# Where layer 0's weights are queued, four normed tiles in layer 1, and four banks for early keys

## The chip, the cores and the metric

The kernel runs on one core of a Trainium2 chip. The core has five engines that each work through their own list of instructions in order: TensorE (PE, with its weight loads PEld), VectorE (DVE), ScalarE (ACT), GpSimd (POOL) and SyncE (SP, which here only issues transfers). They wait for each other through semaphores. ACT, SP and POOL also issue DMA transfers: an instruction in the engine's list starts one, and if that instruction has to wait, everything behind it in the list waits too.

The metric is the device time in microseconds, the median of three runs.

## The reference

A batch of 4 sequences of 256 tokens with 256 features goes through four layers. Each layer is a cross attention to a context of 1601 tokens per sequence and then a feed-forward part, both added to `x`, each on the layer norm of `x`.

```python
x = x + _L0_xattn_ref(_layernorm(x), ctx_2048, mask)
x = x + _L0_ffn_ref(_layernorm(x), ...)      # 32 experts, 8 chosen for each token
x = x + _L1_xattn_ref(_layernorm(x), ctx_2048, ...)   # a decayed mean of the context
x = x + _L1_ffn_ref(_layernorm(x), ...)      # 8 experts, 2 chosen, and a shared expert
x = x + _L2_xattn_ref(_layernorm(x), ctx_2048, ...)   # 16 heads, 4 key-value heads
x = x + _L2_ffn_ref(_layernorm(x), ...)      # 4 experts, 1 chosen
x = x + _L3_xattn_ref(_layernorm(x), ctx_2048, ...)   # 32 heads
x = x + _L3_ffn_ref(_layernorm(x), ...)      # quantized to three weight values
```

Three of these parts matter here. The expert layers 0 and 1 compute, for every token, a weighted sum of the outputs of a few chosen experts, `silu(x Wg) * (x Wu)` times `Wd`. And layer 2's attention needs keys and values of the context, which depend only on the context and not on `x`:

```python
k_ctx = (h_ctx_kv @ wk_ctx).reshape(B, T, NUM_KV_HEADS, HEAD_DIM)
v_ctx = (h_ctx_kv @ wv_ctx).reshape(B, T, NUM_KV_HEADS, HEAD_DIM)
k_ctx = rms_norm(k_ctx, k_norm_w)
```

## The kernel before

**Stages.** The stages run in the order of the layers: layer 0's attention (0 to 141 us in the profile), layer 0's router and token sort (141 to 231), its expert tiles (231 to 376), the way back of its results (376 to 498), layer 1's norms, router, shared expert and expert tiles (498 to 624), their way back (624 to about 668), and from there layer 2's attention, whose first scores come at 694.75. Layer 1's attention is only a mean and two layer norms, and is done inside layer 0's way back.

**An expert layer** works in five steps. `normed` (L106) makes the layer norm of each of the four sequences: VectorE writes a tile `xn` of 128 x 512, ACT issues a write of it to memory (`xd`, L114), PE transposes it into a bank `tp_ln` and VectorE or ACT (in turn, `evac`) copies that to `xnT`. The tiles `xn` come from a pool of two, so the third norm can be written only when the first tile's write to memory has landed. Then the router's products give logits; VectorE finds the chosen experts (`match_replace`, a one-hot `oh`), and `slots` (L524) counts with two products how many tokens each expert has. One-hot products on PE in four parts sort the tokens (L383 to L403). For each tile of 128 sorted tokens, POOL gathers the rows of `xd` by an indirect DMA, PE transposes them, multiplies with the expert's weights, and the result is written to `yd`. There are 95 such tiles in layer 0 and 23 in layer 1. On the way back POOL gathers for each 128 tokens the rows of their chosen experts from `yd` (8 gathers in layer 0, 2 in layer 1) and VectorE adds them to `x` with their gates (L515, L860).

**Layer 0's weights** are two tensors of 32 experts, `w13` (6 MB) and `w2` (3 MB). Eight parts of four experts are loaded by 16 DMAs in a loop ahead of the norms (L337 to L339), all from ACT's list. In the compiled program every DMA from ACT or SP signals on one of eight semaphores in turn, and waits, before it is issued, for the landing of the earlier one on the same semaphore.

**Early keys.** Layer 2's context keys and values of 15 of the 16 pairs of sequence and head group (units) are made ahead of time, as filling work for PE. `l2_early` (L1169) is a generator; each `next` on it, by `fill(n)` (L101), puts one step in. A unit has 7 product steps and 4 turn steps, 11 in all. A product step is four matmuls of two context tiles of 128 rows into one PSUM bank; ACT copies the keys out (`kr_early`, L1200) and the values (`va_early`, six buffers, L1201), and SP stores the values (`vd`). After the seventh, ACT squares the keys (`sq_early`, one buffer), VectorE sums the squares (`ss_early`, L1212), and the keys are scaled (L1216, on `self.scaler`: VectorE on the ways back, otherwise POOL). The turn steps transpose the keys of the unit before on PE, ACT copies them out (`kT_early`, three buffers, L1227), and SP stores them (`kd`). How many steps go where is written in the tables `F0`, `G0`, `F1` and `G1`: 9 for each of the nine rounds of layer 0's way back, 3 for each of the ten of layer 1's.

**PSUM.** In the expert layers eight banks are in four pairs: `tp` and `tpf` (pool `psf`), `gu` (`psg`), `y` (`psy`). The bank of a filling step comes from `self.take`, here the pair `tpf`. The expert tiles use `y` for the last product (`f0y`, `f1y`).

**Order.** A scheduler places each engine's instructions by its own estimate of when they are ready. Those given to `pin` keep their order in the program. It does not follow the text line by line, so an edit can move other instructions as well.

**Into layer 2.** `l2_xattn` (L1245) first loads a mask, a norm weight and rotary tables (L1267 to L1276) from SP's list, and multiplies the tables with the norm weights on VectorE. The tile `wb` has one buffer, so the second of its loads waits until VectorE has used the first. Then come the norm of the first sequence (transposes L1297) with two filling steps, its query products with the remaining ones, and the scores.

Of the kernel before, what the change touches and what calls it, by code (L numbers as in the profile page):

```python
# [11 lines left out]
F32 = mybir.dt.float32  # L12
# [11 lines left out]
P = 128  # L24
B = 4
S = 256
NT = B * S
D = 256
# [8 lines left out]
E0, I0, K0 = 32, 96, 8  # L37
# [3 lines left out]
NH2, NKV2, HD2 = 16, 4, 128  # L41
# [7 lines left out]
F1 = [1, 2, 2, 3]  # L49
G1 = 3  # L50
LN2, Q2, C2 = 2, 2, 6
# [7 lines left out]
class Kernel:  # L59
    def __init__(self, ctx, tc, ins, out):  # L60
        self.ctx, self.tc, self.nc = ctx, tc, tc.nc
        self.i, self.out = ins, out
        self.flip = 0


# [32 lines left out]
    def pin(self, ins):  # L98
        self.tc.keep_in_program_order(ins)

    def fill(self, n):  # L101

        for _ in range(n):
            next(self.early, None)

    def normed(self, ps, fills, xd=None):  # L106


        xT = [self.xnT.tile([P, 2, 512], F32, name=f"xnT{tb}", tag="xnT") for tb in range(2)]
        for b in range(B):  # L110
            xn = self.xn.tile([P, 2, D], F32, name="xn")
            self.layernorm(xn, self.x[b])
            if xd is not None:
                self.nc.scalar.dma_start(xd.rearrange("(b q p) d -> b p q d", p=P, q=2)[b], xn)  # L114
# [199 lines left out]
    def l0_ffn(self, one):  # L314
# [7 lines left out]
        nc, tc = self.nc, self.tc  # L322
# [9 lines left out]
        with ExitStack() as es:  # L332
# [3 lines left out]
            w2 = wp.tile([I0, E0, D], F32, name="f0w2")  # L336
            for e in range(0, E0, 4):  # L337
                nc.scalar.dma_start(w13[:, e : e + 4], self.i["l0_w13"][:, e : e + 4])
                nc.scalar.dma_start(w2[:, e : e + 4], self.i["l0_w2"][:, e : e + 4])  # L339
            src = rt.tile([P, NS], U32, name="f0src")  # L340
# [5 lines left out]
            nc.gpsimd.tensor_scalar(start, tok[:, 0:1], float(P), None, ALU.mult)  # L346
            xT = self.normed(ps, F0[:B], xd)


            lg = products()[:, : 8 * E0].rearrange("p (t e) -> p t e", e=E0)  # L350
            for t in range(8):
                for k in range(2):
                    self.mm(lg[:, t, :], xT[t // 4][:, k, (t % 4) * P : (t % 4 + 1) * P], wr[:, k, :], k == 0, k == 1)
            self.fill(F0[B])
            self.l1_summary()
            l = rt.tile([P, 8, E0], F32, name="l0_l")
# [6 lines left out]
            nc.vector.tensor_single_scalar(oh, oh, GONE, ALU.is_equal)  # L363
            cum, end = self.slots(rt, "f0", E0, oh, products(), low, keep, lambda: self.fill(F0[B + 1]))

            cum1 = rt.tile([P, E0, 8], F32, name="f0cum1")
# [16 lines left out]
            for part in range(4):  # L383
                ones = []
                for t in range(2 * part, 2 * part + 2):
# [9 lines left out]
                    ones.append((t, rows, cols))  # L395
                self.fill(F0[B + 2])
                for t, rows, cols in ones:
                    for r in range(K0):
# [97 lines left out]
    def l0_add(self, two, weights):  # L496
# [3 lines left out]
        slot, gate, yd = self.back0  # L500
        self.scaler = nc.vector
        rows = []
        for t in range(9):
# [16 lines left out]
            if t > 5:  # L520
                next(weights, None)
        self.scaler = nc.gpsimd

    def slots(self, pool, name, ne, oh, ct, low, keep, meanwhile):  # L524
# [126 lines left out]
    def l1_ffn(self, weights):  # L651
# [11 lines left out]
        with ExitStack() as es:  # L663
# [27 lines left out]
            def shared_expert():  # L691

                last = None
                for t in range(9):
# [9 lines left out]
                    if last is not None:  # L704
                        u, h = last
                        tp = ps.tile([P, 3, P], F32, name="f1tps", tag="tp")
                        hT = two.tile([P, 3, P], F32, name="f1hTs")
                        y = ps_y.tile([P, D], F32, name="f1y", tag="y")
                        for m in range(3):
# [116 lines left out]
            def down(n, hT):  # L826
                y = ps_y.tile([P, D], F32, name="f1y", tag="y")
                for m in range(2):
# [16 lines left out]

            self.scaler = nc.vector
            rows = []
            for t in range(10):
# [7 lines left out]
                if t > 1:  # L856
                    xt = self.x[(t - 2) // 2][:, (t - 2) % 2, :]
                    for r in range(K1):
# [4 lines left out]
                        )  # L863
                self.fill(G1)
            self.scaler = nc.gpsimd
# [379 lines left out]
    def l2_xattn(self):  # L1245
# [11 lines left out]
        with ExitStack() as es:  # L1257
# [12 lines left out]
            nc.sync.dma_start(kw, i["l2_knw"].rearrange("o p -> p o"))  # L1270
            tabs = {}
            for n, src, nt in (("l2_qnw", "rope_q", 2), ("l2_knw", "rope_k", 3)):
                rope = one.tile([P, 2, nt, HD2], F32, name=src, tag="qt2", bufs=2)
                nc.sync.dma_start(rope, i[src])
                wb = one.tile([P, HD2], F32, name=n + "b", tag="wb")
                nc.sync.dma_start(wb, i[n].to_broadcast([P, HD2]))  # L1276
                ra = one.tile([P, nt, HD2], F32, name=n + "ra")
# [937 lines left out]
```

## Time and profile before

The profile shows one execution on the chip. Its own time is 2638.45 us.

| What | Value |
|---|---|
| median of three runs | 2638.49 us (2635.17 to 2639.96) |
| profiled execution, its own time | 2638.45 us |
| profiled execution, span from first to last instruction | 2636.7 us |
| mean granted TensorE clock | 0.974 of full speed |
| filling products on PE (`fill<-wkc_early,ctxT`) in the whole span | 189.6 us in 780 rows, two rows for a matmul |
| ACT, stage 376 to 498: idle until a key store has landed (before L1227) | 13.4 us |
| POOL, stage 376 to 498: gathers of layer 0's way back (L506) | 64, from 381.3 to 472.6 us, 3.1 us each to landing |
| loads of layer 0's weights | 8 of 768 KB and 8 of 384 KB |
| loads of layer 1's expert weights (`l_w`) | 6 of 704 KB |

How to read the lines that follow: in the page, each digit of a row is the busy share of one of 40 equal slices of 66 us, in tenths; PEclk is the clock granted to TensorE. In the view by windows a line is a stretch of time, its length, the busy time of each engine with the number of instructions, the granted clock, the busy share of the DMA engines and GB/s. In the timeline a line is a start, a duration, an engine (ACTq and SPq are transfers issued from that engine's list), a source line, the operation and what it writes and reads; in brackets stands how long the engine was idle before it and what ended that. In the view of waits a line is who waited for whom, how long in total, how often, and the longest.

### The profile page before, as it was taken

How to read it: one execution, taken by the hardware profiler on the slowest of the kernel's cores; microseconds unless marked ns; L12 is line 12 of the kernel's file. 1: busy time of each engine (PE TensorE's matmuls, PEld its weight loads, DVE VectorE, ACT ScalarE, POOL GpSimd, SP SyncE). 2: the span in 40 equal slices, each digit the busy share in tenths (PEclk: the TensorE clock that was granted, in tenths of full speed). 3: DMA queues.
4: the chain of work that ended last, by engine and by line, in shares of the span. 5: the costliest groups of instructions: out<-in, count | busy, mean ns of one | idle time of the engine just before them, and what ended most of it. 6: DMA issues, size and time to landing. Idle time of an engine off the chain costs nothing. (4 is left out here: it accounts for less than half of the span.)

```text
span 2636.7 us, 47077 instructions
## 1 busy us (share of the span) xinstructions
PE 2491.9 (95%) x17816; PEld 1517.6 (58%) x17816; DVE 1480.0 (56%) x3039; ACT 1310.9 (50%) x2957; POOL 750.8 (28%) x1030
## 2 busy tenths in 40 slices
PE   7989988898799999999999999998998999999997
PEld 4668967676455555555555555655564544545553
DVE  6344637644587777777777777673334414333323
ACT  2334545433644445444544454442326766757775
POOL 1015646123334343334443434431102001011000
PEclk8989999999999999999999999998999999999998
DMA  5154787615511111111111110004211100000000
GB/s 201 60 199 128 186 174 216 205 56 174 162 38 46 39 37 46 46 38 47 46 46 46 46 46 21 9 1 159 87 66 63 34 2 27 4 3 2 6 6 5
DMA packets 94655, 186.25 MB, mean 71 GB/s; under 512 B 15052, under 2 KB 62864, under 8 KB 93232
## 3 DMA queue, kind: packets, MB, share of 16 engines
q1 hardware_dynamic: 78118, 141.36, 15.8%
q0 software_dynamic: 10416, 28.46, 5.0%
q10 hardware_dynamic: 5898, 13.41, 1.5%
q8 instruction: 145, 2.38, 0.4%
q14 instruction: 78, 0.64, 0.1%
HBM read 136.77 MB, written 46.42 MB: 69 GB/s over the span
## 5 line engine op out<-in xcount | busy, mean ns | idle before, releaser
L1471 ACT ACTIVATE p<-s,nm 128x448 f32<-128x448 f32 (+1 forms) x512 | 326.9, 645 | 423.9 <-DVE nm L1467 259.1
L1932 ACT ACTIVATE e<-s 128x1024 f32<-128x1024 f32 (+1 forms) x448 | 404.2, 960 | 160.8 <-PE s L75 156.1
L75 PE MATMUL s<-kT,qT 128*32 128x448 f32 (+1 forms) x4096 | 470.2, 556 | 10.0 <-ACT p L1471 5.0
L75 PE MATMUL o<-pT,va 128*128 128x256 f32 (+2 forms) x1920 | 432.5, 377 | 6.1 <-DVE pT L1513 6.1
L1507 POOL TENSOR_SCALAR p<-p,rm 128x448 f32<-128x448 f32 (+1 forms) x512 | 323.7, 657 | 369.6 <-DVE rm L1500 339.4
L75 PEld LDWEIGHTS o<-pT,va 128*128 128x128 f32 (+1 forms) x1920 | 345.4, 191 | 93.6 <-issue 51.5
L1513 DVE STREAM_TRANSPOSE pT<-p 128x896 f32<-128x896 f32 (+1 forms) x256 | 283.8, 1127 | 37.1 <-POOL p L1507 33.4
L1467 DVE TENSOR_REDUCE nm<-s 128x2 f32<-128x896 f32 (+1 forms) x256 | 282.6, 1104 | 3.4
L75 PE MATMUL s<-qb,kT 32*128 32x256 f32 (+1 forms) x3328 | 267.7, 405 | 11.0 <-ACT e L1932 11.0
L75 PEld LDWEIGHTS s<-kT,qT 128*32 128x32 f32 x4096 | 123.6, 109 | 265.0 <-issue 222.5
L75 PE MATMUL o<-e,va 128*32 128x256 f32 (+1 forms) x3328 | 236.6, 392 | 1.2 <-DVE os L2029 1.2
L75 PEld LDWEIGHTS s<-qb,kT 32*128 32x128 f32 (+1 forms) x3328 | 163.1, 181 | 105.5 <-issue 75.8
L75 PE MATMUL fill<-wkc_early,ctxT 128*128 128x256 f32 x780 | 189.6, 401 | 11.8 <-ACT kT_early L1227 9.6
L75 PEld LDWEIGHTS fill<-wkc_early,ctxT 128*128 128x128 f32 x780 | 152.1, 199 | 43.1 <-ACT kT_early L1227 15.0
L75 PEld LDWEIGHTS o<-e,va 128*32 128x32 f32 (+1 forms) x3328 | 90.8, 110 | 115.5 <-issue 75.5
L1959 POOL TENSOR_TENSOR x<-x,t 128x32 f32<-128x32 f32 x64 | 14.7, 252 | 439.7 <-DVE t L1954 439.7
L1464 DVE TENSOR_TENSOR s<-s,mask 128x128 f32<-128x128 f32 (+1 forms) x256 | 83.1, 325 | 67.1 <-PE s L75 62.3
L410 POOL DMA_INDIRECT f0xr<-f0xd,f0src x95 | 92.3, 972 | 51.3 <-PE f0tph L467 43.2
L1359 POOL TENSOR_TENSOR qo<-qo,qt 128x512 f32<-128x512 f32 x32 | 40.7, 1273 | 230.6 <-DVE rm L1500 139.4
L1471 ACT ACTIVATION_READ_ACCUMULATOR p<-s,nm 128x1 f32 x512 | 101.7, 199 | 0.0
L1200 ACT COPY kr_early<-fill 128x256 f32<-128x256 f32 (+1 forms) x105 | 37.3, 355 | 97.9 <-PE fill L75 97.7
L75 PE MATMUL f2gu<-f2wgu,f2xsT 128*128 x176 | 84.3, 603 | 0.6 <-ACT f2xsT L72 0.3
(510 smaller groups left out, 3503.7 us busy)
## 6 DMA issues: line engine op xcount, KB each, us to landing
ctxT<-in_ctxT SPq DMA_DIRECT2D x10, 1664.0 KB
f0yd<-f0ys SPq DMA_DIRECT2D x95, 128.0 KB
vd<-va_early SPq DMA_DIRECT2D x90, 128.0 KB
kd<-kT_early SPq DMA_DIRECT2D x45, 256.0 KB
kT<-kd SPq DMA_DIRECT2D x15, 768.0 KB
va<-vd SPq DMA_DIRECT2D x15, 768.0 KB
wq<-in_l_wq SPq DMA_DIRECT2D x16, 512.0 KB
wo<-in_l_wo SPq DMA_DIRECT2D x16, 512.0 KB
```

What stands on the lines that cost most here:

```text
L75: self.nc.tensor.matmul(out, lhsT, rhs, start=start, stop=stop, **kw)
L410: nc.gpsimd.indirect_dma_start(out=t, out_offset=None, in_=xd[:, :], in_offset=bass.IndirectOffsetOnAxis(ap=src[:, n : n + 1], axis=0),)
L1200: nc.scalar.copy(kr[:rows, m : m + n, :], tp[:rows, :n, :HD2])
L1359: nc.gpsimd.tensor_tensor(o1, o1, t2, ALU.add)
L1464: nc.vector.tensor_tensor(sv, sv, mask[:, 2 * c : 2 * c + 2, : nt - CT, :].rearrange("p n t i -> p n (t i)"), ALU.add)
L1467: nc.vector.tensor_reduce(nm[:, 2 * c : 2 * c + 2], s[:, :, : nt * 32], AX.X, ALU.max, negate=True)
L1471: nc.scalar.activation(p[:, n, : nt * 32], s[:, n, : nt * 32], AF.Exp, bias=nm[:, e : e + 1], accum_out=sm[:, e : e + 1],)
L1507: nc.gpsimd.tensor_scalar(p[:, n, : nt * 32], p[:, n, : nt * 32], r[:, e : e + 1], 1.0, ALU.mult, ALU.mult)
L1513: nc.vector.transpose(pT[:, 2 * c : 2 * c + 2, :nt, :].rearrange("p n t i -> p n (t i)"), p[:, :, : nt * 32])
L1932: nc.scalar.activation(e[:kr, :, :n, :], s[t][:kr, :, :n, :], AF.Exp, scale=1.0 / math.sqrt(HD3))
L1959: nc.gpsimd.tensor_tensor(xt, xt, t[:, q], ALU.add)
```

## The change

- Layer 0's 16 weight loads leave their place ahead of the norms. A generator `load` issues them in eight parts of two, the even parts from ACT's list and the odd ones from SP's, all pinned. Two parts are put in behind the norms, two behind the router's products, two behind the slot counts, and the last two in the first two rounds of the sort.
- `normed` takes a pool. In layer 1 this is the pool `f1r`, with four buffers for `xn`; layer 0 keeps two.
- `wide_take` hands out four banks for filling steps in turn, the pair `tpf` and the pair `y`. It is used in both ways back. The tiles `y` are declared 512 wide, a whole bank, with the same number of buffers.
- `G1` becomes a table: 9 steps in the first round of layer 1's way back, then 3 three times, then 2. The sum stays 30.
- The six loads of layer 2's mask and tables move from SP's list to ACT's.

```diff
-G1 = 3
+G1 = [9, 3, 3, 3, 2, 2, 2, 2, 2, 2]
...
+    def wide_take(self):
+
+        self.flip4 = not self.flip4
+        if self.flip4:
+            return self.psf[0].tile([P, 512], F32, name="fill", tag="tpf")
+        return self.psf[2].tile([P, 512], F32, name="filly", tag="y")
...
-            xn = self.xn.tile([P, 2, D], F32, name="xn")
+            xn = pool.tile([P, 2, D], F32, name="xn", bufs=B) if pool else self.xn.tile([P, 2, D], F32, name="xn")
...
-            for e in range(0, E0, 4):
-                nc.scalar.dma_start(w13[:, e : e + 4], self.i["l0_w13"][:, e : e + 4])
-                nc.scalar.dma_start(w2[:, e : e + 4], self.i["l0_w2"][:, e : e + 4])
+            def load():
+
+                for n, e in enumerate(range(0, E0, 4)):
+                    queue = nc.sync if n % 2 else nc.scalar
+                    self.pin(queue.dma_start(w13[:, e : e + 4], self.i["l0_w13"][:, e : e + 4]))
+                    self.pin(queue.dma_start(w2[:, e : e + 4], self.i["l0_w2"][:, e : e + 4]))
+                    yield
...
             xT = self.normed(ps, F0[:B], xd)
+            next(loads)
+            next(loads)
...
             self.fill(F0[B])
+            next(loads)
+            next(loads)
             self.l1_summary()
...
             cum, end = self.slots(rt, "f0", E0, oh, products(), low, keep, lambda: self.fill(F0[B + 1]))
+            next(loads)
+            next(loads)
...
                 self.fill(F0[B + 2])
+                next(loads, None)
...
-                y = ps_y.tile([P, D], F32, name="f0y", tag="y")
+                y = ps_y.tile([P, 512], F32, name="f0y", tag="y")[:, :D]
...
+        take = self.take
+        self.take = self.wide_take
...
-            xT = self.normed(ps, F1[:B], xd)
+            xT = self.normed(ps, F1[:B], xd, rt)
...
+            self.take = self.wide_take
...
-                self.fill(G1)
+                self.fill(G1[t])
...
-            nc.sync.dma_start(mask, i["mask2"])
+            nc.scalar.dma_start(mask, i["mask2"])
...
-                nc.sync.dma_start(rope, i[src])
+                nc.scalar.dma_start(rope, i[src])
```

More of the change, by code (lines that the diff above doesn't have):

```diff
@@ L63, in __init__ @@
         self.flip = 0
+        self.flip4 = False
     def evac(self, out, in_):
@@ L104, in fill, with normed @@
             next(self.early, None)
-    def normed(self, ps, fills, xd=None):
+    def normed(self, ps, fills, xd, pool=None):
         xT = [self.xnT.tile([P, 2, 512], F32, name=f"xnT{tb}", tag="xnT") for tb in range(2)]
         for b in range(B):
-            xn = self.xn.tile([P, 2, D], F32, name="xn")
+            xn = pool.tile([P, 2, D], F32, name="xn", bufs=B) if pool else self.xn.tile([P, 2, D], F32, name="xn")
             self.layernorm(xn, self.x[b])
-            if xd is not None:
-                self.nc.scalar.dma_start(xd.rearrange("(b q p) d -> b p q d", p=P, q=2)[b], xn)
+            self.nc.scalar.dma_start(xd.rearrange("(b q p) d -> b p q d", p=P, q=2)[b], xn)
             self.fill(fills[b])
@@ L336, in l0_ffn @@
             w2 = wp.tile([I0, E0, D], F32, name="f0w2")
-            for e in range(0, E0, 4):
-                nc.scalar.dma_start(w13[:, e : e + 4], self.i["l0_w13"][:, e : e + 4])
-                nc.scalar.dma_start(w2[:, e : e + 4], self.i["l0_w2"][:, e : e + 4])
+            def load():
[4 more added lines that the diff above has]
+                    yield
+            loads = load()
             src = rt.tile([P, NS], U32, name="f0src")
@@ L522, in l0_add @@
         self.scaler = nc.gpsimd
+        self.take = take
     def slots(self, pool, name, ne, oh, ct, low, keep, meanwhile):
@@ L707, in shared_expert @@
                         hT = two.tile([P, 3, P], F32, name="f1hTs")
-                        y = ps_y.tile([P, D], F32, name="f1y", tag="y")
+                        y = ps_y.tile([P, 512], F32, name="f1y", tag="y")[:, :D]
                         for m in range(3):
@@ L826, in down @@
             def down(n, hT):
-                y = ps_y.tile([P, D], F32, name="f1y", tag="y")
+                y = ps_y.tile([P, 512], F32, name="f1y", tag="y")[:, :D]
                 for m in range(2):
@@ L1266, in l2_xattn @@
             mask = one.tile([P, 8, 3, 32], F32, name="mask2")
-            nc.sync.dma_start(mask, i["mask2"])
+            nc.scalar.dma_start(mask, i["mask2"])
             kw = one.tile([P, 1], F32, name="kw")
-            nc.sync.dma_start(kw, i["l2_knw"].rearrange("o p -> p o"))
+            nc.scalar.dma_start(kw, i["l2_knw"].rearrange("o p -> p o"))
             tabs = {}
@@ L1273, in l2_xattn @@
                 rope = one.tile([P, 2, nt, HD2], F32, name=src, tag="qt2", bufs=2)
-                nc.sync.dma_start(rope, i[src])
+                nc.scalar.dma_start(rope, i[src])
                 wb = one.tile([P, HD2], F32, name=n + "b", tag="wb")
-                nc.sync.dma_start(wb, i[n].to_broadcast([P, HD2]))
+                nc.scalar.dma_start(wb, i[n].to_broadcast([P, HD2]))
                 ra = one.tile([P, nt, HD2], F32, name=n + "ra")
```

## The prediction

> **What bounds the kernel now.** I read the page first: which engine is full, and in which slices it is not.
>
> ```profile
> span 2636.7 us, 47077 instructions
> PE 2491.9 (95%) x17816; PEld 1517.6 (58%) x17816; DVE 1480.0 (56%) x3039; ACT 1310.9 (50%) x2957; POOL 750.8 (28%) x1030
> PE   7989988898799999999999999998998999999997
> ...
> PEclk8989999999999999999999999998999999999998
> ```
>
> TensorE is busy for 95% of the span. A slice is 66 us; outside the first and the last, every 7 and all but two of the 8s for PE lie in slices 3 to 11 (132 to 726 us). That is the mixture-of-experts work of layers 0 and 1, which the change touches. Elsewhere PE is full, so a gain must come from idle PE time or from a slow PE clock in these slices. The second view is the busy time of each engine by stage (window, length, then PE, PEld, DVE, ACT, POOL, then clock, DMA share, GB/s):
>
> ```profile
> 141.00:157.60 16.60, 4.93 (x30) 4.16 (x28) 1.36 (x4) 0.61 (x2) 2.49 (x10) 0.74 0.97 333
> 157.60:169.00 11.40, 11.39 (x41) 10.21 (x42) 3.42 (x25) 4.50 (x10) 0.00 (x0) 0.50 1.03 360
> 376.00:498.20 122.20, 106.72 (x485) 83.57 (x483) 88.11 (x203) 65.59 (x174) 68.03 (x87) 0.96 0.68 212
> 498.20:526.00 27.80, 22.04 (x100) 18.46 (x101) 10.27 (x32) 8.92 (x23) 0.00 (x0) 0.82 0.74 245
> 624.00:694.70 70.70, 55.63 (x251) 43.35 (x249) 31.68 (x78) 37.19 (x96) 26.80 (x31) 0.90 0.76 243
> 694.70:2636.00 1941.30, 1878.07 (x14840) 1032.54 (x14839) 1120.85 (x2093) 1022.27 (x2144) 509.63 (x749) 0.98 0.11 37
> ```
>
> PE is idle 11.7, 15.5, 5.8 and 15.1 us in the stages at 141, 376, 498 and 624, and for 11.4 us it runs at half clock. The third view, the timeline, says what ends these times. At 141 us:
>
> ```profile
> 145.52 0.34 ACTq L338 DMA_DIRECT2D f0w<-in_l_w  x1
> ...
> 156.59 0.33 ACTq L339 DMA_DIRECT2D f0w<-in_l_w  x1
> 156.97 0.59 ACT L72 COPY xnT<-tp_ln 128x512 f32<-128x512 f32 x1 [18.13 <-DMA f0w<-in_l_w]
> 157.61 3.62 PE L75 MATMUL f0gu<-r,xnT 128*128 128x32 f32 x16 [11.68 <-ACT xnT L72]
> ```
>
> ScalarE issues all 16 weight loads in one go. Eight go out 0.5 us apart; from the ninth on they come in pairs 3.33 us apart, because each waits for a load eight before it to land. The copy that PE needs is queued behind them. Two answers of the view of waits, for the two ways back (376 to 498, 624 to 695):
>
> ```profile
> PE fill L75 <- ACT kT_early L1227: 8.2, 11, 1.8
> PE fill L1225 <- ACT kT_early L1227: 4.6, 8, 1.7
> ```
>
> ```profile
> PE fill L1225 <- ACT va_early L1201: 7.4, 1, 7.4
> ACT sq_early L1211 <- DVE ss_early L1212: 6.4, 1, 6.4
> ```
>
> In the first, many short waits of the early keys for a PSUM bank that ScalarE has not emptied; in the second, one long wait: ScalarE's square stands for a VectorE sum that is queued behind additions of gathered rows. Last, the norms of layer 1:
>
> ```profile
> 510.92 0.73 DVE L93 TENSOR_SCALAR xn<-x,ln_mv,ln_rs 128x256 f32<-128x256 f32 x2 [5.99 <-DMA f1xd<-xn]
> ```
>
> The third norm waits until the first one's tile has been written to memory, behind 4.3 MB of weights (six loads of 704 KB, issued 498.80 to 505.39).
>
> **The change part by part.** All of it is priced in the profiled execution: 2638.45 us, that is the span of 2636.7 and 1.75 around it. It stands 0.04 under the median of 2638.49, so the saving goes straight onto the median.
>
> *1. Layer 0's weights.* In the changed program's order the last two normed copies stand ahead of the weights on ScalarE. The idle 11.68 us go. The half clock after it goes too: 11.4 us at 0.50 is 5.7 us, 17.4 in all. Here a rule disagrees: the Trainium skill, "TensorE: Matmul & The Clock Gate", section "What's actually happening", says that about 3.4 us of sustained work bring the full clock back, which makes the loss 3.4 x 0.5 = 1.7 us. The row shows 0.50 for 11.4 us, so I take 5.7 and note that the sum would be 4 lower by the rule. A second rule speaks against the edit: "DMA: Bandwidth & Descriptors", section "Issuing engines are not separate DMA queues", says that several issuing engines share the same 16 DMA engines and save only the issue time. The row agrees on the transfer: 360 GB/s at a share of 1.03 on one queue, so 9216 KB (9.4 MB) take about 26 us on two queues as well. By the rule the edit is worth 16 issues of some 0.4 us, about 6 us; by the row ScalarE stood from 141 to 156.97, because issue waited for landing. I take the row. Not free: PE now comes to the slot counts (L532) with only three fill matmuls (1.3 us) after the router, while VectorE needs 166.38 to 170.18, 3.8 us, from the logits to the one-hot: 2.5 us of new wait. The loads among the value stores on SP delay those stores by a part's transfer, 3.3 us; six buffers at some 1.7 us a step cover it. ScalarE's last two parts stand close together, the second waits for the first: up to 3.3 us, partly under PE's sorting matmuls; I charge 1. The last part is issued near 200 us and its experts run after 300, so no tile waits. Sum 17.4 - 2.5 - 1 = 13.9, **14** (10 to 17).
>
> *2. Four banks, first way back.* Idle 15.5 us plus a clock of 0.96 over 122 us (4.9 us) make a ceiling of 20. The waits between turns and products (0.36 and 0.52 us a unit, 7.4 units of 11 steps in 81 steps: 6.5 us) are bank waits alone and go. The longer ones (up to 1.8 us) come when ScalarE stands for landings of key stores (13.4 us of its idle time there). Those stay, but two more banks hold two more steps of 8 rows at 0.217 us, 3.5 us of PE work, against ScalarE waits of 2.3 to 4.0. Next in line are the gathers: 64 at 1.25 us from start to start, 80 us from 381.3 to 461, 85 us into the stage, before PE's 102 us of work (106.72 at a clock of 0.96); and VectorE, 88 of 122 us busy and in order, with sums, scalings and additions that wait for other engines. I take two thirds: **13** (6 to 20).
>
> *3. Four normed tiles.* Norms 1 and 2 are 3.49 us apart (500.34, 503.83). At that pace norm 4 stands at 510.8 instead of 518.15: 7.3 us, and less half clock after the gap (4.0 us at 0.62: 1.5). The slow writes are then waited for by the gather, first at 555, so they stay hidden. **8** (5 to 11).
>
> *4. Second way back: nine steps first, four banks, tables on ScalarE.* In the new order VectorE's sums stand behind two gathered additions instead of five, so most of the 7.4 us goes. PE then runs 32 us of fills from 624.8: two units of 12.7 (48 rows at 0.217 us, 0.4 for the short last tile, 13 transposes in 1.9) and a remainder of 6.3. So layer 2's first transpose comes near 656.5 and the last product near 662.5 instead of 678.62. From there to the first scores took 16.1 us (to 694.75), which I keep: 678.6, a gain of 16. The six table loads cost ScalarE 6 x 0.4 = 2.4 us where it is half idle; the last waits for a VectorE product behind two gathers, and key and value copies queue behind it, and PE for them. SP stood 8 us at it before (633.5 to 641.40). With four banks I charge 5: **11** (0 to 18).
>
> *5. At nothing:* wider `y` tiles (same buffer count), total fills (81 and 30 as before), the POOL tables behind 24 gathers (needed 100 us later).
>
> Sum 14 + 13 + 8 + 11 = 46 us: 2638.5 - 46 = **2592.5**.
>
> **The rivals.**
> *A: banks are not what holds the fills.* ScalarE's waits for landings remain and more banks only shift them; part 2 gives 6, part 4 nothing: 14 + 6 + 8 = 28, **2610.5**. For it: 13.4 us of landing waits in the stage. Against: PE's own waits there are at most 1.8 us. Chance 0.20.
> *B: everything packs.* All ceilings, 17 + 20 + 11 + 18 = 66: **2572.5**. For it: gathers and ScalarE (66 of 122 us) have room. Against: VectorE is 72% busy in order, with cross waits. Chance 0.14.
> *C: slower, weights late.* The parts now stand in two queues among value stores and behind fills. Eight parts for 145 us of experts (231 to 376) are 18 us of tiles a part, so from a start at 217 the last part is needed near 343. It decides from a landing at 389 on (46 us late): 9.4 MB from 147 us in 242 us, 39 GB/s. At the 38 GB/s of slice 12 they take 248 us, until 395, 52 us late: **2644.5**, and each us of landing is a us more. Against: 360 GB/s measured, and the last issue near 200. Chance 0.04.
> *D: no effect,* other chains take over at once: **2638**, chance 0.02.
>
> **How the numbers follow.** The forecast has 0.60. Its own range, each part half way to its ends, is about 2580 to 2605 (14, 13, 8, 11 against 12, 9.5, 6.5, 5.5 and 15.5, 16.5, 9.5, 14.5). The range must reach into A and B: 2575 to 2615 leaves most of B below, C and D and a little of A above, about 0.2. One measurement can't tell 0.2% (5.3 us) from no change. Faster is forecast, A and B: 0.94; same 0.02; slower 0.04.
>
> **What would show it.** Right: no PE gap over 3 us between 141 and 231 and a clock near 1.0 there, experts starting near 217 instead of 231; the first way back about 109 us long instead of 122; no landing before L93 in layer 1's norms; first scores near 649. Wrong: PE waiting for `f0w` landings in the experts (C); key-store landings with PE waits as long as before (A); layer 2's preparation standing idle after the last product for more than 16 us.

## The result, and the profile after

The changed kernel takes **2616.95 us** (median of six runs, 2609.97 to 2621.88), the kernel before 2636.97 in the same comparison: a ratio of 0.9926 (95% interval 0.9914 to 0.9939). That is 20 us faster where 46 were forecast (2592.5), and just above the stated range of 2575 to 2615.

The profiled execution is the quickest of the six. From its page, the span, the busy times, and the rows by slice of TensorE's busy time and clock:

```profile
span 2608.2 us, 47024 instructions
PE 2472.6 (95%) x17800; PEld 1512.2 (58%) x17816; DVE 1473.9 (57%) x3039; ACT 1307.1 (50%) x2955; POOL 751.9 (29%) x1030
...
PE   7989978999899999999999999998998999999997
...
PEclk8999999899999999999999999998999999999998
```

Counted from 1, slices of 65 us: the clock of slice 3 (130 to 196 us) rose from 8 to 9, and PE rose by one in slices 8, 10 and 11, the norms and the second way back. But in slice 6 (326 to 391 us), where the first way back begins, PE fell from 8 to 7, and the clock of slice 8, where it ends, from 9 to 8. The view of busy time by stage, for the changed kernel (window, length, PE, PEld, DVE, ACT, POOL, clock, DMA share, GB/s):

```profile
141.40:219.70 78.30, 70.48 (x362) 58.72 (x360) 38.42 (x112) 33.05 (x82) 19.77 (x29) 0.98 0.61 192
219.70:364.70 145.00, 138.58 (x854) 126.07 (x855) 72.12 (x214) 73.56 (x286) 87.45 (x91) 1.00 0.72 169
364.70:477.80 113.10, 93.59 (x439) 78.58 (x438) 76.32 (x176) 56.38 (x153) 69.66 (x86) 0.91 0.69 217
477.80:547.60 69.80, 67.22 (x321) 52.58 (x320) 37.89 (x151) 27.55 (x76) 4.94 (x6) 0.93 0.39 126
605.50:670.20 64.70, 54.71 (x254) 43.06 (x252) 34.54 (x83) 37.39 (x99) 26.88 (x31) 0.92 0.78 257
```

In the third line PE is idle for 19.5 us, where it was 14.2 before in the same bounds. All stages below are bounded in the trace in this way: **sort** from the first router product of layer 0 to the first product of an expert tile; **first way back** from the last expert product to the last row added to `x` (L538); **norms** from there to the first expert tile of layer 1; **second way back** from layer 1's last expert product to layer 2's first scores.

| Kernel | sort | experts 0 | first way back | norms | second way back | to first scores |
|---|---|---|---|---|---|---|
| before | 89.5 | 146.3 | 111.9 | 76.9 | 71.1 | 694.8 |
| changed | 77.9 | 145.0 | 113.3 | 69.7 | 64.8 | 670.3 |
| forecast of the difference | -14 | 0 | -13 | -8 | -11 | -46 |
| measured difference | -11.6 | -1.3 | +1.4 | -7.2 | -6.3 | -24.5 |

Each stage time here and below comes from one profiled execution.

The forecast failed above all in one place, the first way back: 14.4 of the 21.5 us that are missing up to the first scores. Its timeline in the changed kernel, where PE has its two long gaps:

```profile
383.04 0.95 POOL L529 DMA_INDIRECT f0yt<-f0yd,f0slot  x1 [0.31 <-issue]
...
389.02 0.23 POOL L1231 MEMSET kr_early<- 32x128 f32 x1
389.28 0.52 ACT L1236 ACTIVATE sq_early<-kr_early 128x384 f32<-128x384 f32 x1 [6.62 <-POOL kr_early L1231]
...
390.43 2.07 PE L76 MATMUL filly<-wkc_early,ctxT 128*128 128x256 f32 x4 [7.27 <-ACT kT_early L1252]
...
400.16 0.30 POOL L654 CAST f1lane<-f1li 128x128 f32<-128x128 int32 x1
...
400.50 0.17 DVE L800 TENSOR_SCALAR f1first<-f1lane 1x23 f32<-1x23 f32 x1 [16.71 <-POOL f1lane L654]
400.59 0.53 DVE L1237 TENSOR_REDUCE ss_early<-sq_early 128x3 f32<-128x384 f32 x1
...
401.16 0.31 ACT L80 ACTIVATE ss_early<-ss_early,eps 128x13 f32<-128x13 f32 x1 [10.20 <-DVE ss_early L1237]
...
402.09 2.50 PE L76 MATMUL filly<-wkc_early,ctxT 128*128 128x256 f32 x5 [5.51 <-ACT kT_early L1252]
```

The numbers in brackets are idle times, and they lead from PE to POOL twice. The first gap: PE waits for ScalarE's copy, the copy stands behind a square in ScalarE's list, the square waits for a 0.2 us memset that clears the padding of the keys, and the memset stands behind 16 gathers on POOL, some 1.25 us each. The second: VectorE stands for 16.7 us at `f1first`, a tiny instruction of layer 1's sort that reads the table `f1lane`; POOL makes that table only after 24 gathers, and the sums of squares that the fills need are queued behind `f1first`. The same tile in the trace of before:

```profile
L630 POOL CAST f1lane<-f1li x1: 304/304/304, 378.3 to 378.3; 128x128 f32<-128x128 int32 x1
L776 DVE TENSOR_SCALAR f1first<-f1lane x1: 166/166/166, 378.6 to 378.6; 1x23 f32<-1x23 f32 x1
...
who waited for it (us, times):
  DVE f1first L776: 0.9, 1
```

There the table was made at 378.3, ahead of the first gather (381.33), and `f1first` read it 0.3 us later, not 100 us later. So the trace of before already showed how early this reader stands.

### The profile page after: what moved, and what is told of

Same layout as the page of the kernel before. It is cut to its first block, busy times and chain, and to the rows that moved or that the text cites. A ratio compares the mean times of both kernels' runs of the same rounds, so it can differ in the third digit from the quotient of the medians.

```text
span 2608.2 us, 47024 instructions
## 1 busy us (share of the span) xinstructions
PE 2472.6 (95%) x17800; PEld 1512.2 (58%) x17816; DVE 1473.9 (57%) x3039; ACT 1307.1 (50%) x2955; POOL 751.9 (29%) x1030
## 5 line engine op out<-in xcount | busy, mean ns | idle before, releaser
L76 PE MATMUL s<-qb,kT 32*128 32x256 f32 (+1 forms) x3328 | 267.6, 404 | 13.2 <-ACT e L1957 11.0
L76 PEld LDWEIGHTS o<-e,va 128*32 128x32 f32 (+1 forms) x3328 | 90.5, 110 | 115.0 <-issue 74.9
L76 PE MATMUL fill<-wkc_early,ctxT 128*128 128x256 f32 (+1 forms) x532 | 130.7, 394 | 8.2 <-ACT kT_early L1252 7.8
L76 PEld LDWEIGHTS fill<-wkc_early,ctxT 128*128 128x128 f32 (+1 forms) x532 | 102.0, 196 | 26.2 <-ACT kT_early L1252 10.3
L529 POOL DMA_INDIRECT f0yt<-f0yd,f0slot x64 | 66.8, 1044 | 47.5 <-DMA vd<-va_early 16.3
```

The source lines that it names most:

```text
L76: self.nc.tensor.matmul(out, lhsT, rhs, start=start, stop=stop, **kw)
L529: nc.gpsimd.indirect_dma_start(out=yt, out_offset=None, in_=yd[:, :], in_offset=bass.IndirectOffsetOnAxis(ap=slot[:, t, r : r + 1], axis=0),)
```

## The experiments

Eleven of the eighteen runs fell on chips where the kernel before takes 2636 to 2639 us, as above; the runs e5 to e8 and e16 to e18 fell on two where it takes 2682.5 and 2682.7. Ratios are each to the kernel before on the same chip; stage times are compared only within one kind of chip, except the sort, which is alike on both (with the weights as in the change 77.9 to 86.6 us on the first kind, 81.8 to 86.5 on the other). "Both" is the changed kernel with the edits of e2 and e3. An interval of a ratio reaches 0.001 to 0.002 to either side, 3 to 5 us, so a stage's gain or loss of 3 us is hardly seen in the total.

| Run | sort | first way back | norms | second way back | median us | ratio (95%) |
|---|---|---|---|---|---|---|
| changed | 77.9 | 113.3 | 69.7 | 64.8 | 2616.95 | 0.9926 (0.9914-0.9939) |
| e1 two tiles | 82.5 | 104.3 | 78.7 | 65.8 | 2619.65 | 0.9942 (0.9927-0.9957) |
| e2 f1first on POOL | 82.8 | 104.8 | 68.4 | 66.9 | 2614.51 | 0.9913 (0.9900-0.9926) |
| e3 memset on VectorE | 83.5 | 111.4 | 66.8 | 67.4 | 2618.57 | 0.9932 (0.9918-0.9947) |
| e4 both | 81.9 | 98.7 | 68.2 | 67.0 | 2608.67 | 0.9892 (0.9877-0.9907) |
| e10 both, again | 82.1 | 98.1 | 66.7 | 67.1 | 2605.76 | 0.9886 (0.9865-0.9906) |
| e9 changed, two banks | 79.4 | 124.9 | 70.7 | 68.9 | 2634.32 | 0.9985 (0.9974-0.9997) |
| e11 both, two banks | 81.9 | 109.5 | 68.7 | 68.1 | 2620.26 | 0.9936 (0.9917-0.9955) |
| e12 both, tables on SP | 85.3 | 98.3 | 68.0 | 64.4 | 2606.86 | 0.9879 (0.9859-0.9898) |
| e13 both, flat steps | 81.7 | 97.6 | 65.0 | 70.1 | 2606.03 | 0.9891 (0.9876-0.9906) |
| e14 both, two banks second | 86.6 | 98.7 | 69.7 | 69.5 | 2610.91 | 0.9901 (0.9885-0.9916) |
| e15 both, one queue | 86.0 | 97.7 | 66.6 | 66.9 | 2606.73 | 0.9892 (0.9879-0.9906) |
| *other kind of chip:* e18 changed | 82.4 | 139.4 | 69.5 | 71.5 | 2659.96 | 0.9908 (0.9892-0.9923) |
| e5 before, weights only | 82.6 | 147.3 | 78.6 | 70.7 | 2674.03 | 0.9966 (0.9954-0.9978) |
| e6 both, two banks | 86.5 | 149.5 | 66.7 | 74.0 | 2675.85 | 0.9971 (0.9960-0.9982) |
| e7 both, tables on SP | 81.8 | 132.6 | 66.7 | 68.0 | 2649.13 | 0.9875 (0.9860-0.9891) |
| e8 both, small squares | 83.5 | 134.6 | 66.7 | 71.3 | 2653.95 | 0.9883 (0.9863-0.9902) |
| e16 both, late weights | 76.2 | 136.4 | 68.2 | 71.5 | 2648.14 | 0.9877 (0.9859-0.9896) |
| e17 e16, tables on SP | 76.2 | 138.5 | 68.3 | 66.6 | 2642.01 | **0.9844** (0.9830-0.9857) |

### What moved the table, and what the two waits cost (e1 to e4)

```diff
# e1, in the changed kernel
-            xT = self.normed(ps, F1[:B], xd, rt)
+            xT = self.normed(ps, F1[:B], xd)
# e2
-            nc.vector.tensor_scalar(first, lane[:1, :NS], float(P), None, ALU.mult)
+            nc.gpsimd.tensor_scalar(first, lane[:1, :NS], float(P), None, ALU.mult)
# e3 (e4: e2 and e3)
-            nc.gpsimd.memset(kr[96:, CT2, :], 0.0)
+            nc.vector.memset(kr[96:, CT2, :], 0.0)
```

> The changed kernel with one part undone: layer 1's norms write their tiles from the old pool of two. In its compiled order layer 1's sort tables stand ahead of the first gather on POOL again, as before the change; in the changed kernel they stand behind 24 gathers. Theory T (the first way back lost its gain to waits for POOL: VectorE's f1first stood 16.7 us for a table queued behind gathers, ScalarE's square 6.6 us for a padding memset queued behind gathers): the wait for the table goes, the way back from the last expert product to the last added row takes about 106 us instead of 113.1; the norms lose what part 3 gained, 69.8 becomes about 77 us; the total stays within 3 us of the changed kernel. Rival R (ScalarE's waits for the landings of key stores hold the fills, the waits for POOL only replaced them): the way back stays at 111 to 114 us, the norms cost 7 us, the total is about 7 us above the changed kernel.

> The changed kernel with one instruction moved: layer 1's f1first is computed on POOL, right behind its table, instead of on VectorE. T: VectorE's wait of 16.7 us goes, and with it the PE gap of 5.5 us at 397 us; the padding memset still holds PE for some 7 us; the way back shrinks from 113.1 to about 107 us, the total by 4 to 8 us against the changed kernel. R: another wait ends at the same place, the way back changes by less than 2 us.

> The changed kernel with the padding memset of the early keys on VectorE instead of POOL. T: ScalarE's square no longer waits for POOL, the PE gaps of 7.3 us at 383 us and 3.2 us at 468 us go; but VectorE still stands at f1first until the tables behind 24 gathers are made (near 400 us), so PE runs into that wait earlier: the total falls by 3 to 7 us, the way back to about 108 us. R: less than 2 us.

> The changed kernel with both edits, f1first on POOL and the padding memset on VectorE. T: no PE gap over 2 us is left in the first way back, it takes about 100 us (the 11 to 13 us of the prediction), the total falls by 10 to 15 us against the changed kernel. R: landings of key stores and VectorE's sums take over, the way back stays above 108 us and the total falls by less than 5 us.

**e1** undoes part 3 alone, and the table is ahead of the gathers again. VectorE's waits at the start of its way back (370 to 415 us), who waited for whom, total, times, longest:

```profile
DVE f1first L800 <- POOL f1lane L654: 0.9, 1, 0.9
```

So it was the four tiles in the pool `f1r` that sent the tables behind the gathers: the way back falls by 9.0 us, the norms rise by 9.0, and the total stays where it was (2619.65 against 2616.95). Part 3 by itself is worth nothing in this kernel. Why the larger pool makes POOL's tables later was not tried.

**e2** leaves everything and takes only VectorE's wait away: 8.5 us less in the way back, the gap near 400 gone. The total fell by less than that (2614.51; the intervals of the two ratios overlap). **e3** missed: alone it brings 1.9 us, because PE then runs into the wait for `f1first` at once, in one gap of 13.2 us. **e4** has both, and the way back takes 98.7 us. PE's waits in it (364 to 480 us), first in e4, then in the changed kernel:

```profile
PE filly L76 <- ACT kT_early L1252: 3.6, 2, 2.3
PE fill L76 <- ACT kT_early L1252: 3.1, 5, 0.7
```

```profile
PE filly L76 <- ACT kT_early L1252: 13.3, 3, 7.3
PE fill L76 <- ACT kT_early L1252: 4.5, 3, 3.2
```

The same waits, but no long one any more (2.3 us at most, where nothing over 2 was expected). Table 8.5 us and memset 6.4 us (104.8 to an average of 98.4 in e4 and e10) make 14.9 us. The shares depend on the order: with the memset gone first, it is 1.9 us for the memset (e3) and 13.0 for the table (111.4 to 98.4). The rival, that landings of key stores would take over, would have kept the way back above 108 us: it falls. e4 and e10 lie 28.6 and 33.0 us below their kernels before, the changed kernel 20.0; T's 10 to 15 us came out as 9 to 13.

### What four banks are worth (e6, e9, e10, e11)

```diff
# e9 in the changed kernel, e6 and e11 in "both": first way back
         take = self.take
-        self.take = self.wide_take
```

> The kernel with f1first on POOL and the memset on VectorE, but only two banks for filling steps in the first way back. T (four banks are worth what part 2 said, 6 to 20 us, once nothing else holds the engines): the first way back grows from 98.7 to 106 us or more, the total by 6 to 13 us. Rival A (banks don't hold the fills, the two waits for POOL were the whole matter): the way back grows by less than 3 us.

> The changed kernel with two banks for filling steps in the first way back instead of four, the two waits for POOL left in. T (in the changed kernel the waits for POOL eat what the four banks give): the way back and the norms of layer 1 together stay within 5 us of the changed kernel's 183.1 on a chip like its own, and the total within 5 us of it. Rival (four banks gave their 13 us, and the waits for POOL cost as much beside them): 8 us or more above the changed kernel, a ratio to the kernel before of 0.9955 or more.

> f1first on POOL and the memset on VectorE, once more, as the partner of the runs of this call. T: a ratio to the kernel before of 0.986 to 0.992 on either chip, the first way back near 99 us on a chip where the transfers land in 2 to 5 us; on a chip like the one of the last four runs (133 to 150 us for the way back) near 133 us.

> The same with two banks in the first way back. T: with the waits for POOL gone, two banks cost 8 us or more of the first way back against the partner of this call, and as much of the total. Rival A: less than 3 us; the difference of 22 to 27 us in the last four runs then belonged to that chip's slow landings.

With the waits gone two banks cost 11.4 us of the way back (e11 against e10). **e9** contradicts what I expected: I thought that the waits for POOL had eaten the banks' gain. But two banks cost 11.6 us there as well (124.9 against 113.3), with this wait on PE (one line was taken out, so L1249 is the changed kernel's L1250):

```profile
PE fill L1249 <- ACT kT_early L1251: 16.4, 6, 14.3
```

and with this one on ScalarE:

```profile
405.55 0.52 ACT L1235 ACTIVATE sq_early<-kr_early 128x384 f32<-128x384 f32 x1 [13.81 <-DVE ss_early L1236]
```

With two banks PE has two steps fewer to run on with, so the wait for the table costs it 14.3 us in one piece. The memset was made at 393.08 there, and ScalarE does not wait for it at all; that wait grew long only with four banks. The two effects add up: four banks brought 11.5 us; the waits took 14.9 with four banks and 15.4 with two (e9 against e11). On the other kind of chip e6 lies 22 us above e8 and 27 above e7, in the same direction.

### The second way back (e7, e8, e12, e13, e14)

```diff
# e7, e12 (and e17), in "both": all six loads of layer 2's mask and tables
-                nc.scalar.dma_start(rope, i[src])
+                nc.sync.dma_start(rope, i[src])
# e8, in "both"
-            for m in range(0, NM, 5):
-                n = min(5, NM - m)
-                sq = e2.tile([P, 5, HD2], F32, name="sq_early", bufs=1)
+            for m in range(0, NM, 3):
+                n = min(3, NM - m)
+                sq = e2.tile([P, 3, HD2], F32, name="sq_early", bufs=2)
# e13, in "both"
-                self.fill(G1[t])
+                self.fill(3)
# e14, in "both": second way back
-            self.take = self.wide_take
```

> The kernel with f1first on POOL and the memset on VectorE, with layer 2's six table loads on SP as before the change. If the queue matters (SP standing 8 us for the single buffer of the norm weights, with the key and value stores behind it): the second way back grows from 67.0 by 3 to 8 us. If what matters is that tables, query weights and context share the DMA engines with the gathers (7 us to landing): it stays within 2 us of 67.0, and the PE gap of 5 us stays.

> The kernel with f1first on POOL and the memset on VectorE, and with the squares of the early keys in pieces of three tiles and two buffers instead of five tiles and one. If ScalarE's wait for VectorE's sum of squares, queued behind additions of gathered rows, makes the PE gap in the second way back: the gap of 5 us shrinks to 3 us or less, the second way back from 67.0 to about 64 us, and the first way back gains 1 to 3 us too. If PE waits for something else there (landings of value stores, a bank): no change beyond 1 us; ScalarE pays two squares more a unit, about 0.5 us each.

> The same with four banks and with layer 2's table loads on SP. If the queue of the loads decides the second way back: 3 us or more above the partner of this call there. If the shared DMA engines decide it: within 2 us of the partner; below it by 1 to 3 us if ScalarE's issues are what costs.

> f1first on POOL, the memset on VectorE, and three filling steps in each round of the second way back instead of nine first. If the nine steps first are what gave the gain of part 4: the second way back grows from 67.0 to 70 us or more, with a PE wait of 6 us or more for sums behind additions. If they gave nothing (landings of the gathers, 7 us, hold the first additions whatever stands around them): within 1.5 us of 67.0.

> f1first on POOL, the memset on VectorE, and two banks for filling steps in the second way back, four in the first. If banks matter there as in the first way back (11 us over 81 steps, so 0.14 us a step, 4 us over 30 steps): the second way back grows to 70 us or more. If the one long wait for gathered rows is all: within 1.5 us of 67.0.

The nine steps first are worth 3.0 us here (70.1 against an average of 67.1, with a PE wait of 7.5 us, as expected), the four banks 2.4 (69.5, short of the 70 expected), and the tables on ScalarE cost 2.7 (e12 64.4 against 67.1; on the other kind of chip e7's 68.0 against e8's 71.3, and e17's 66.6 against e16's 71.5). The first two have one run each and are small: with the changed kernel's edits in this stage it took 64.8 (changed) to 68.9 us (e9), and the medians of e10, e12 and e13 lie within 1.1 us. Of e12's three answers the last came true in size, but, by the traces, not for its reason; e7's 68.0 stands where its second answer put it, on a chip where this stage is otherwise 4 us longer. The timeline of the changed kernel at this place:

```profile
611.80 0.41 SPq L136 DMA_DIRECT2D ctxT<-in_ctxT  x1
...
611.98 1.08 POOL L876 DMA_INDIRECT f1yt<-f1yd,f1slot  x1 [4.40 <-DMA kd<-kT_early]
...
619.57 0.48 DVE L885 SCALAR_TENSOR_TENSOR x<-f1yt,f1gate,x 128x256 f32<-128x256 f32 x1 [7.14 <-DMA f1yt<-f1yd,f1slot]
...
621.64 0.81 DVE L1237 TENSOR_REDUCE ss_early<-sq_early 128x5 f32<-128x640 f32 x1
...
622.84 0.74 ACT L1236 ACTIVATE sq_early<-kr_early 128x640 f32<-128x640 f32 x1 [7.07 <-DVE ln_st L90]
...
624.16 1.12 PE L1250 MATMUL filly<-ident,kr_early 128*128 128x128 f32 x4 [5.61 <-ACT va_early L1226]
```

The load of a context of 1664 KB is issued with the first gather. The gather's rows are there only 7.6 us after its start, VectorE's addition waits for them, the sum of squares behind it, ScalarE's square (its 7.07 us are put down to the instruction next to that sum), and in the end PE 5.6 us. In e12 the tables stand in SP's queue ahead of that load and hold it back:

```profile
603.54 0.95 POOL L876 DMA_INDIRECT f1yt<-f1yd,f1slot  x1 [7.17 <-DMA kd<-kT_early]
...
607.07 0.48 DVE L885 SCALAR_TENSOR_TENSOR x<-f1yt,f1gate,x 128x256 f32<-128x256 f32 x1 [1.26 <-DMA f1yt<-f1yd,f1slot]
...
614.77 0.43 SPq L136 DMA_DIRECT2D ctxT<-in_ctxT  x1
```

There the rows are added 3.5 us after the gather's start, the context goes out 11 us after it, and the longest PE gap of the stage is 2.4 us. All twenty profiles split in this way. In fifteen the context load goes out between 3.6 us before and 1.3 us after the first gather, and the first addition comes 6.1 to 8.3 us after the gather's start; in the five others (before, e5, e7, e12, e17) it goes out 11.2 to 13.0 us after the gather, and the addition comes after 3.4 to 5.2. But no run moved the context load without the tables, so that it is the load that counts is read from traces, not shown by a run. By this reading the stalled SP queue of the kernel before was not only a loss: it kept a large load away from the gathers. **e8** brought nothing that can be seen (71.3 against e16's 71.5, a gap of 4.5 instead of 5.6 us): ScalarE still stands 3.4 us before a later square (7.1 us in e16).

### Layer 0's weights (e5, e15, e16)

```diff
# e5: the kernel before with the generator load and its calls, nothing else
# e15, in "both"
-                    queue = nc.sync if n % 2 else nc.scalar
+                    queue = nc.scalar
# e16 (and e17), in "both": behind the slot counts; the sort's four rounds then issue one part each
-            next(loads)
-            next(loads)
```

> The kernel before with part 1 alone (layer 0's weights in parts on two queues behind the norms). T (part 1 is worth somewhat less than the 14 us forecast, since PE's waits for ScalarE behind slow key-store landings and the low clock after them came in its place): router and sort take 78 to 84 us instead of 89.5, with PE idle for 8 us instead of 14; the total falls by 7 to 12 us against the kernel before. Rival: the loads now fall on the sort's stores and on the first tiles, and most of it is given back: less than 5 us.

> f1first on POOL, the memset on VectorE, and all eight parts of layer 0's weights on ScalarE's queue, behind the norms. If the second queue matters (each issue waits for the landing eight issues before, and copies queue behind it): router and sort take 86 us or more instead of 82, with PE idle for 11 us or more. If only the place behind the norms matters: 80 to 84 us.

> f1first on POOL, the memset on VectorE, and the last four parts of layer 0's weights issued one in each of the sort's four rounds instead of two right behind the slot counts. If the key stores' slow landings behind the weights make the PE gap of 2 to 3 us near 188 us and the clock of 0.7 to 0.8 after it: the gap shrinks below 1 us, router and sort take 79 us or less instead of 82. If the gap only moves with the parts: 81 to 85 us.

Alone on the kernel before, part 1 takes 8.5 us off the total and leaves 8.0 us of idle PE in the sort (e5), as expected. **e15** has the size expected for one queue (86.0 us, 12.3 us of idle PE instead of 8.0 to 8.4 in e4 and e10, at the same clock of 0.92), but not its reason. No weight load waits long in it; ScalarE's list has another order:

```profile
159.67 0.42 ACT L450 ACTIVATE l_l<-l_l 128x256 f32<-128x256 f32 x1 [6.34 <-DVE l_l L449]
```

In e4 the copies of two filling steps stand ahead of this instruction, in e15 behind it, and PE stands 3.7 us for them. So what a second queue is worth stays open, and the total shows nothing. What was left over of part 1 is seen in the changed kernel's second profile, e18, on ScalarE:

```profile
181.15 0.69 ACT L1252 ACTIVATE kT_early<-fill,kw_early 128x512 f32<-128x512 f32 x1
188.62 0.37 ACT L1252 ACTIVATE kT_early<-fill,kw_early 128x128 f32<-128x128 f32 x1 [6.78 <-DMA kd<-kT_early]
188.64 0.35 ACTq L349 DMA_DIRECT2D f0w<-in_l_w  x1
```

Weight parts are still under way, and a key store whose landing ScalarE needs lands late; PE then stands for 2.0 us at 187.1. The two stretches from 141.5 to 219 us, of e18 and then of e16, whose last four parts go out later:

```profile
141.50:180.00 38.50, 34.39 (x185) 29.51 (x183) 21.58 (x86) 18.25 (x43) 6.05 (x14) 1.00 0.56 175
180.00:219.00 39.00, 36.21 (x155) 28.25 (x156) 16.27 (x26) 11.77 (x31) 10.66 (x12) 0.78 0.56 189
```

```profile
141.50:180.00 38.50, 34.29 (x168) 29.02 (x168) 20.94 (x85) 16.60 (x40) 5.07 (x10) 0.96 0.53 169
180.00:219.00 39.00, 37.38 (x197) 31.02 (x197) 15.56 (x30) 17.27 (x45) 13.26 (x14) 1.00 0.71 223
```

With the later parts the gap is gone, the clock is 1.00 instead of 0.78, and 197 matmuls fit where 155 did. The sort takes 76.2 us in e16 and in e17, 13.3 less than before, where the nine other versions of "both" on two queues took 81.7 to 86.6. In e16's total this is not seen (0.9877 against 0.9886 and 0.9892 in e10 and e4).

### The version that takes all of it (e17, e18)

> The kernel of the run before with layer 2's table loads on SP as well. If both effects are real they add: a second way back of about 64.5 us and a total 2 to 5 us below e10's ratio, that is 0.987 to 0.988 of the kernel before. If they are within the noise of a run: 0.9886 again.

> The changed kernel itself, as the partner of this call: a ratio of 0.9914 to 0.9939 to the kernel before, as measured, and 8 to 12 us above the two runs before it; its router and sort near 82 us, as in the kernels that share its order there, rather than the 77.9 of its first profile (the clock differs between executions).

e17 is the changed kernel with four mends: `f1first` on POOL, the memset on VectorE, the last four weight parts later, the tables on SP. Its ratio of 0.9844 lies below the expected 0.987: 40.7 us under the kernel before, and 18 under the changed kernel on the same chip (8 to 12 were expected for e16 and e17; e16 came to 11.8). Against e7 (0.9875), which lacks only the later weights, the intervals lie apart. The second way back took 66.6 us where 64.5 were expected, and e18's ratio of 0.9908 came out just under the 0.9914 expected.

## Why the prediction was wrong, point by point

**The step that failed** is the last of the sum: "*5. At nothing:* ... the POOL tables behind 24 gathers (needed 100 us later)". The move was seen and put at nothing, because the sort of layer 1 comes 100 us later. But one reader of the table, `f1first`, does not depend on that sort, and stands early in VectorE's list. An engine works through its list in order, so its wait is everyone's who is behind it: 8.5 us in e2, 13.0 once the memset is out of the way (e3 to e4). The padding memset is a second wait for POOL, which no term of the sum has: 6.4 us more (e4). It came 24.1 us after the last expert product before (401.38 against 377.24) and 24.3 us after (389.02 against 364.73), unmoved; before, ScalarE waited 1.3 us for it, now 6.6, and with two banks in e9 not at all. The four banks brought PE to it sooner, so a faster engine met an event that had not become faster. Without the two waits the stage takes 98.7 and 98.1 us (e4, e10) instead of the 111.9 of before, which is the gain of 13 that part 2 promised.

**Part 2, four banks: right.** Forecast 13, measured 11.4 and 11.6. Rival A, banks that don't hold, is out, though the total came near its 2610.5. The gain was given back in the same stage.

**Part 3, four tiles: right in its stage, wrong in its reach.** Forecast 8, measured 7.2 in the norms, and 9.0 lost in the first way back (e1), since its larger pool is what moved the tables.

**Part 1, weights: right mechanism, a term too small.** Forecast 14, measured in the sort 11.6 in the first profile, 6.7 to 10.1 in the four others with the same order there (e1, e2, e9, e18), and alone 8.5 of the total. The 11.7 us gap went, and the wait at the slot counts was 1.7 us instead of 2.5. In the first profile PE's busy time from 141 us to the first expert tile fell from 76.0 to 70.5 us, about the 5.7 of the low clock that the row gave; the estimate of 1.7 from the rule in the Trainium skill, "TensorE: Matmul & The Clock Gate", section "What's actually happening", would have been too little. In e18 PE was busy for 74.9 us: a low clock behind the weights took most of it back. Mis-sized was "up to 3.3 us, partly under PE's sorting matmuls; I charge 1": the wait for a key store behind the weights costs 1.4 to 3.5 us of PE near 188 us, and 5.5 us or more with the low clock around it (76.2 in e16 and e17 against 81.7 or more). The 6 us that the prediction estimated by the Trainium skill's rule of two queues ("DMA: Bandwidth & Descriptors", section "Issuing engines are not separate DMA queues") were too little for the whole edit; what the second queue adds to the later place, the rule's own matter, no run here shows.

**Part 4, second way back: half.** Forecast 11, measured 6.3, and 4.0 in e4 and e10. The last early product came 8 us earlier relative to the experts' end (46.9 after it, 55.1 before), not 16: I took "most of the 7.4 us goes", and a PE gap of 5.6 us stayed, with gathered rows that land in a median of 7.2 us instead of 3.1 before. With the tables back on SP the gap is 2.4 us and the stage 2.7 us shorter (e12); the other missing part of the forecast stays open.

The five parts as measured in the profile make 11.6 + 1.3 - 1.4 + 7.2 + 6.3 = 25 us (0.4 were lost before the sort); the medians differ by 20, and the executions of one kernel by 12. The profiled one is the quickest, with the shortest sort of the five that share its order.

## What to carry to other kernels

When a compiled order moves small work behind a long row of gathers or loads, ask who reads it first in any engine's list, not when the stage that it is made for begins; a tiny early reader stops everything behind it. Price each part also by what it makes meet: the four banks were worth what their own rows said, and the stage lost it again to a memset and a table that had hardly been in anybody's way before. And undo each part singly: a part worth nothing by itself (here the four tiles) may hide a gain and a loss of the same size.

## What the runs showed of the hardware

- **Two kinds of chip, two times.** The kernel before takes 2636 to 2639 us on some chips and 2682.5 and 2682.7 on two others. For the changed kernel (e18 against its first profile) the difference lies in the stages with many transfers: experts of layer 0 155.8 against 145.0 us, first way back 139.4 against 113.3, second 71.5 against 64.8; the last stage, 1941.7 against 1938.0, differs by 0.2%. In e18's first way back ScalarE stands for 27.5 us in five waits whose end its trace can't name, and these transfers' landing times are not in it, so why stays open.
- **The same instructions, another clock.** Five profiles have one and the same order of instructions in the sort (changed, e9, e18, e1, e2). They took 77.9, 79.4, 82.4, 82.5 and 82.8 us, at a granted clock of 0.98, 0.96, 0.90, 0.92 and 0.90. All have PE gaps of 1.1 us near 180 us and of 1.9 to 3.3 us near 188; e16 and e17 have neither gap, and a clock of 1.00 from 180 to 219 us. The clock of e18 in three stretches:

```profile
184.50:194.80 10.30, 8.32 (x21) 5.36 (x20) 2.97 (x6) 1.66 (x5) 1.41 (x3) 0.50 0.89 294
194.80:208.40 13.60, 13.60 (x74) 11.48 (x73) 6.67 (x13) 5.61 (x15) 0.74 (x1) 1.00 0.46 149
208.40:215.30 6.90, 6.57 (x24) 4.79 (x23) 4.08 (x4) 2.28 (x5) 4.17 (x5) 0.51 0.24 86
```

The first low stretch begins ahead of the gap at 187.1, and the second follows 13.6 us of work without a pause. In the first profile only 183.7 to 187.2 is low (0.51). So low clock and short gaps occur together here, but these gaps don't fix how long it lasts, and the stage's length in one execution is uncertain by 5 us.
